# Attention layer and four-way state-space layer on one core: one frame for the sums of D, turned copies in 2 KB runs ordered during the scans

## The chip, the cores and the metric

The kernel runs on one core of a Trainium2 chip. The metric is device time in microseconds (us), from start to end of one execution. The engines are PE (TensorE, matrix products; PEld is its weight load), DVE (VectorE), ACT (ScalarE), POOL (GpSimd) and SP (SyncE, which issues most DMAs). Each works through its own queue in order. "DVEq", "POOLq" and the like are an engine's sequencer: waits and issues.

## The reference, cut to what matters

```python
# layer 0, on x of (B, H, W, C) = (8, 128, 128, 128)
q, k, v = split(x @ w_qkv)                      # 4 heads of 32, N = H*W tokens
q = softmax(q over the 32) / sqrt(32);  k = softmax(k over N)
context = einsum('bhdn,bhen->bhde', k, v)
out = einsum('bhde,bhdn->bhen', context, q) @ w_out + b_out
x1 = layernorm(out) + x

# layer 1, on x1
xb, z = split(x1 @ Win)                         # 256 channels each
u = silu(conv3x3_depthwise(xb))                 # in the code: xb
xs = [u by rows, the same reversed, u by columns, the same reversed]   # K = 4 orders
dt, B, C = split(xs_flat @ Wxproj)              # 8 + 1 + 1 rows per image and order
delta = softplus(dt_weight @ dt + dt_bias)
# the (image, order) axis of u, B, C and dt is reshaped from (8, 4) to (4, 8), so output image o, slot s
# takes image o // 4 + 2 * s in order o % 4
h[t] = exp(delta[t] * A) * h[t-1] + delta[t] * u[t] * B[t];  y[t] = h[t] * C[t] + u[t] * D
y = y_0 + reversed(y_1) + turned(y_2) + turned(reversed(y_3))
out = (layernorm(y * silu(z)) * gamma + beta) @ Wout
```

"Turned" means that the two axes of the 128 x 128 image change places.

## The kernel before

The kernel has three parts in sequence. All images are held with channels on the 128 partitions. The layout NAT runs through an image column by column (the input arrives with w ahead of h), TURN row by row.

**layer0** does the attention image by image, in `ORDER`, with 32 groups of 512 tokens (4 columns) per image. While one image is in `attend`, the next is in `context`; the stages of both are interleaved by hand in `image`, and `in_order` keeps each engine's instructions in the written order. Between images, `gate` projects x to z for the gating of layer 1: per group two matrix products, a silu on ACT, and two stores of 256 KB to `zs`; after that (or, for images that are not turned, in eight pieces meanwhile) it loads the image after the next. For images with `ORDER[b] % K >= 2` DVE first makes a turned copy `v` of the group. `finish` makes x1 and stores two groups at a time. The last two images have their gate groups spread through the last pass.

**layer1_front** takes x1 through the projection, the 3 x 3 depthwise convolution and silu, in `SEQ` order of images (4, 6, 5, 7, 0, 1, 2, 3), 16 steps of 1024 tokens (8 columns) each, for both halves c of 256 channels. Two of the nine taps are on PE (`taps_pe`), three on ACT with POOL adding (`taps_act`), four on DVE (`taps_dve`). `rows` and `keep_rows` make the ten rows of dt, B and C; `by_b` multiplies u by B and stores it in NAT order to `ubs`. A whole image of u stays in SBUF (`ures`). Eight steps later and on, `turn` copies it turned, in pieces of 16 rows by 64 columns, two pieces (`ka`, `kb`) a step, and `store_turned` writes each piece to the TURN half of `ubs`. `copy_on` says which engine copies. `split_step` turns the ten rows (`turn_rows`) and splits them in both orders into three bf16 parts (`split`), two rows at a time.

`sum_d` makes D * u on ACT. The sums of D over the four images that meet in one output are gathered in DRAM: images 4 to 7 go to `gts` in blocks of 8 x 8, and images 0, 1 read them back (`load_sum`), add them on POOL, and store the result to `gs`, to which images 2, 3 add by an accumulating DMA from POOL's queue (`add_sum`).

**layer1_scan** runs over 8 output images x 4 slots x 16 units of 1024 tokens. A unit makes delta (PE, ACT), the product with u (`weigh`, on POOL, in place in `ubt`), the scan itself (DVE), the product by C (`emit`, DVE) and the addition to y (`gather` on DVE, `add` on POOL). The slot at place 0 starts an image's y; meanwhile the image before leaves: `gate`, moments, `project`, `store`. `add_d` adds the sums of D to y by an accumulating DMA from POOL's queue. In `step` the order of every engine is again written out by hand.

Two lines carry much of what follows: the product in place, and a turned piece's 64-element runs in DRAM.

```python
nc.gpsimd.tensor_tensor(ubt[n][:, c, :], ubt[n][:, c, :], sp.pop((n, c)), ALU.mult)      # weigh
nc.sync.dma_start(dst[:, 16 * i : 16 * i + 16, hf * HALF : hf * HALF + HALF], turned.pop(k))   # store_turned
```

Of the kernel before, what the change touches and what calls it, by code (L numbers as in the profile page):

```python
# [16 lines left out]
P = 128  # L17
# [11 lines left out]
ORDER = (2, 3, 6, 7, 4, 5, 0, 1)  # L29
# [11 lines left out]
def split3(eng, parts, x, copy):  # L41

    for j in range(3):
        copy(parts[j], x)
        if j < 2:
            eng.tensor_tensor(x, x, parts[j], ALU.subtract)
# [31 lines left out]
def layer0(ctx: ExitStack, tc, xT, w_qkv, w_out, b_out, gamma, beta, win, x1, zs):  # L78
# [68 lines left out]
    def gate_group(b, g):  # L147

        v = group(b, g)
        if ORDER[b] % K >= 2:  # L150
            v = wp.tile([P, GW, P], F32, name="v", tag="o", bufs=3)
            nc.vector.tensor_copy(
                v, xs[b % 2].rearrange("p w h -> p h w")[:, g * GW : (g + 1) * GW, :]
            )
        for c in range(NC2):
            pz = ps.tile([P, GW, P], F32, name="pz", tag="ps")
            nc.tensor.matmul(pz, wz[:, c * P : c * P + P], v, start=True, stop=True)
            z = wp.tile([P, GW, P], F32, name="z", tag="k", bufs=7)
            nc.scalar.activation(z, pz, AF.Silu)
            dst = zs[ORDER[b], c][:, g * GN : g * GN + GN]  # L160
            nc.sync.dma_start(dst, z.rearrange("p w h -> p (w h)"))

    def gate(b):

        turned = ORDER[b] % K >= 2
        more = b + 2 < B
        for g in range(NG):
            gate_group(b, g)
            if more and not turned and g % 4 == 3:
                load(b + 2, [g // 4])  # L170
        if more and turned:
# [89 lines left out]
    def attend(b):  # L261
# [61 lines left out]
        def finish(g):  # L323
# [4 lines left out]
            if g % 2 == 1:  # L328
# [55 lines left out]
def layer1_front(ctx: ExitStack, tc, x1, win, conv_w, conv_b, wxp, d_par, ubs, xds, xps, gts, gs):  # L384
# [19 lines left out]
    ON_PE = ((1, -1), (1, 1))  # L404
    ON_ACT = ((-1, -1), (-1, 0), (-1, 1))
    ON_DVE = ((0, -1), (0, 0), (0, 1), (1, 0))
# [3 lines left out]

    ident = const.tile([P, P], F32, name="ident1")
    make_identity(nc, ident)
    cw = const.tile([P, NC2, 9], F32, name="cw")
# [45 lines left out]
    SEQ = (4, 6, 5, 7, 0, 1, 2, 3)  # L459

# [3 lines left out]
    accs, sums, pxs, prs, pbs, gls, dus = {}, {}, {}, {}, {}, {}, {}  # L464
# [42 lines left out]
    def taps_act(n, c):  # L507
        for j, d in enumerate(ON_ACT):
# [4 lines left out]
            nc.scalar.activation(t, at(n, c, *d), AF.Copy, scale=cw[:, c, tap(*d) : tap(*d) + 1])  # L513
# [5 lines left out]
    def taps_dve(n, c):  # L519
        acc = accs[n, c]  # L520
        nc.vector.tensor_tensor(acc, sums.pop((n, c)), acc, ALU.add)  # L521
        for d in ON_DVE:
            nc.vector.scalar_tensor_tensor(  # L523
                acc, at(n, c, *d), cw[:, c, tap(*d) : tap(*d) + 1], acc, ALU.mult, ALU.add
            )
# [27 lines left out]
    def by_b(n):  # L553

        b, g = place_of(n)
        dst = ubs[b, NAT].rearrange("c p l -> p c l")
# [6 lines left out]
    def sums_at(n, c):  # L563
        b, g = place_of(n)
        i = NCH - 1 - g if b // 2 % 2 == 1 else g
        if b >= 4:
            return gts[b % 2, c, :, i].rearrange("p e q -> p (e q)")
        return gs[b % 2, c][:, i * CH : i * CH + CH]

    def load_sum(n, c):  # L570
        b, g = place_of(n)
        if b // 2 == 0:
            gls[n, c] = gl = wp.tile([P, CH], F32, name="gl", tag="d", bufs=2)
            nc.sync.dma_start(gl.rearrange("p (e q) -> p e q", e=NCH), gts[b % 2, c, :, :, g])

    def sum_d(n):
        b, g = place_of(n)
        s = b // 2
        for c in range(NC2):
            u = ures[:, c, g * CH : g * CH + CH]  # L580
            if s == 0:
                dus[n, c] = t = wp.tile([P, CH], F32, name="du", tag="tb", bufs=4)
                nc.scalar.activation(t, u, AF.Copy, scale=sd[:, s, c : c + 1])
                gl = gls.pop((n, c)).rearrange("p (e h) -> p h e", h=8)
                tw = t.rearrange("p (w h) -> p w h", w=CW)
                nc.gpsimd.tensor_tensor(tw, tw, gl, ALU.add)
                continue
            dus[n, c] = t = wp.tile([P, CH], F32, name="du", tag="d", bufs=2)
            dst = t[:, ::-1] if s % 2 == 1 else t
            if s >= 2:  # L590
                u = u.rearrange("p (w i h) -> p w i h", w=CW, h=8)
                dst = dst.rearrange("p (i w h) -> p w i h", w=CW, h=8)
            nc.scalar.activation(dst, u, AF.Copy, scale=sd[:, s, c : c + 1])

    def store_sum(n):
        s = place_of(n)[0] // 2
        if s % 2 == 0:
            for c in range(NC2):
                nc.sync.dma_start(sums_at(n, c), dus.pop((n, c)))

    def add_sum(n):
        s = place_of(n)[0] // 2
        if s % 2 == 1:
            for c in range(NC2):
                nc.gpsimd.dma_start(sums_at(n, c), dus.pop((n, c)), accum_op=ALU.add)
# [6 lines left out]
    def turn(k, copy, tag, bufs):  # L612
        m, r = divmod(k, COPIES)
        b, hf = SEQ[m // 2], m % 2
        c, i = divmod(r, COPIES // NC2)
        turned[k] = t = wp.tile([P, 2 * 8, HALF], F32, name="turned", tag=tag, bufs=bufs)
        copy(t, uturn[:, c, 16 * i : 16 * i + 16, hf * HALF : hf * HALF + HALF])

    def store_turned(k):
# [3 lines left out]
        dst = ubs[b, TURN][c].rearrange("p (h w) -> p h w", w=W)  # L623
        nc.sync.dma_start(dst[:, 16 * i : 16 * i + 16, hf * HALF : hf * HALF + HALF], turned.pop(k))

    def dve_copy(out, x):
        nc.vector.scalar_tensor_tensor(out, x, 1.0, x, ALU.mult, ALU.max)

    def copy_on(n, second):
        s = place_of(n)[0] // 2 if n < N else 2  # L630
        if s == 0:
            return nc.scalar.copy if second else dve_copy if n % 2 else nc.gpsimd.tensor_copy
        if s % 2 == 1 and second:
            return dve_copy if n % 2 else nc.scalar.copy
        return nc.gpsimd.tensor_copy
# [4 lines left out]
    def load_rows(q, r0, rows, tag, bufs):  # L640
        x = wp.tile([P, rows, H], F32, name="xw", tag=tag, bufs=bufs)
        xws[q, r0] = x
# [3 lines left out]
    def turn_rows(q, r0, rows, tag, bufs):  # L646
        x = xws[q, r0]
        pt = (pm if rows <= 4 else pj).tile([P, rows, P], F32, name="ptx", tag="m" if rows <= 4 else "pj")
        for j in range(rows):
            nc.tensor.transpose(pt[:, j, :], x[:, j, :], ident)  # L650
        y = wp.tile([P, rows, W], F32, name="xh", tag=tag, bufs=bufs)
        nc.scalar.copy(y, pt)
        xws[q, r0, TURN] = y

    def split(q, r0, rows, order, eng, tag, bufs):
        v = xws.pop((q, r0, TURN) if order == TURN else (q, r0))
        p = wp.tile([P, 3, rows, P], BF16, name="parts", tag=tag, bufs=bufs)
        split3(eng, [p[:, j] for j in range(3)], v, dve_copy if eng is nc.vector else eng.tensor_copy)
        parts.append((q, r0, rows, order, p))

    def store_parts():
        while parts:
            q, r0, rows, order, p = parts.pop()
            dst = xps[SEQ[q], order].rearrange("j r (a e) -> a j r e", e=P)
# [3 lines left out]
    def split_step(n):  # L668
# [6 lines left out]
        eng = nc.vector if place_of(n)[0] // 2 == 0 else nc.gpsimd  # L675
        if odd:
            turn_rows(q, 2 * j, 2, "sy", 1)
            split(q, 2 * j, 2, NAT, eng, "sq", 1)
        else:
            if j:  # L680
                split(q, 2 * j - 2, 2, TURN, eng, "sq", 1)
# [3 lines left out]
    def step(n):  # L685
# [6 lines left out]
        if ka >= 0:  # L692
            turn(ka, copy_on(n, False), "tc", 2)
# [15 lines left out]
        if live:  # L709
            for c in range(NC2):  # L710
                load_sum(n, c)
        if ka - 1 >= 0:
            store_turned(ka - 1)
# [566 lines left out]
```

## Time and profile before

| | |
|---|---|
| median of 3 runs | 9476.79 us (9473.5 to 9477.35) |
| profiled execution | 9477.74 us, span 9475.9 us |
| busy share of PE, DVE, ACT, POOL | 67%, 86%, 75%, 79% |
| DMA packets | 1,510,245, of them 799,444 under 512 bytes |
| bytes moved | 1784 MB, mean 188 GB/s |

The profile is of one execution. A group's row gives line, engine, operation, tiles (out<-in), shapes and count; then the busy us, the mean ns of one, and after the second bar the idle us just before its instructions and what ended them. "Windows" give the busy time of each engine between two times. The DMA share is that of 16 DMA engines.

### The profile page before, as it was taken

How to read it: one execution, taken by the hardware profiler on the slowest of the kernel's cores; microseconds unless marked ns; L12 is line 12 of the kernel's file. 1: busy time of each engine (PE TensorE's matmuls, PEld its weight loads, DVE VectorE, ACT ScalarE, POOL GpSimd, SP SyncE). 2: the span in 40 equal slices, each digit the busy share in tenths (PEclk: the TensorE clock that was granted, in tenths of full speed). 3: DMA queues.
4: the chain of work that ended last, by engine and by line, in shares of the span. 5: the costliest groups of instructions: out<-in, count | busy, mean ns of one | idle time of the engine just before them, and what ended most of it. 6: DMA issues, size and time to landing. Idle time of an engine off the chain costs nothing. (4 is left out here: it accounts for less than half of the span.)

```text
span 9475.9 us, 89695 instructions
## 1 busy us (share of the span) xinstructions
PE 6389.1 (67%) x24352; PEld 3122.5 (33%) x24352; DVE 8149.5 (86%) x8046; ACT 7125.4 (75%) x8034; POOL 7474.3 (79%) x4743
## 2 busy tenths in 40 slices
PE   8999999898989887788633644637345363543636
PEld 5555555564333332233200311304023040320403
DVE  6667765563999999999789999999999999999996
ACT  5556655567888887788678888888878888888884
POOL 3445544455789987788769999999999999999997
PEclk9999999999999998899855755758566585665857
DMA  2331233314598898999955958769586685967858
GB/s 92 134 134 71 106 134 132 133 63 152 180 230 244 231 231 229 233 232 224 226 158 171 273 154 228 223 181 264 158 238 203 190 256 166 247 187 201 248 163 214
DMA packets 1510245, 1784.08 MB, mean 188 GB/s; under 512 B 799444, under 2 KB 1025364, under 8 KB 1501552
## 3 DMA queue, kind: packets, MB, share of 16 engines
q1 hardware_dynamic: 1456496, 1577.01, 53.5%
q0 software_dynamic: 53248, 201.34, 11.4%
q8 instruction: 199, 3.26, 0.1%
q14 instruction: 302, 2.47, 0.1%
HBM read 1085.92 MB, written 692.12 MB: 188 GB/s over the span
## 5 line engine op out<-in xcount | busy, mean ns | idle before, releaser
L963 POOL TENSOR_TENSOR ubt<-ubt,sp 128x1024 f32<-128x1024 f32 x1024 | 2458.0, 2458 | 160.0 <-ACT sp L956 96.1
L952 PE MATMUL px<-rows,dtw 128*128 128x512 bf16 x2048 | 953.6, 565 | 2238.4 <-DVE y L1013 1069.2
L515 POOL TENSOR_TENSOR tap<-tap 128x1024 f32<-128x1024 f32 x512 | 1261.4, 2468 | 234.3 <-ACT tap L513 209.2
L523 DVE SCALAR_TENSOR_TENSOR acc<-xb,cw,acc 128x1024 f32<-128x1024 f32 x1024 | 1320.6, 1290 | 54.0 <-ACT xb L492 1.7
L956 ACT ACTIVATE sp<-px 128x1024 f32<-128x1024 f32 x1024 | 1046.2, 1024 | 418.1 <-PE px L952 351.0
L1021 POOL TENSOR_TENSOR y<-y,ubt 128x512 f32<-128x512 f32 x768 | 1155.3, 1550 | 146.0 <-DVE ubt L994 144.9
L505 PE MATMUL acc<-xi,wt 128*128 128x512 f32 x2048 | 1028.1, 648 | 314.3 <-ACT ures L530 314.3
L973 DVE TENSOR_TENSOR_SCAN ubt<-px,ubt 128x1024 f32<-128x1024 f32 x512 | 1176.9, 2332 | 27.4 <-POOL ubt L963 20.3
L971 DVE TENSOR_TENSOR_SCAN ubt<-px,ubt 128x1024 f32<-128x1024 f32 x512 | 1178.4, 2332 | 13.1 <-POOL ubt L963 6.0
L952 PEld LDWEIGHTS <-dtw 128*128 128x128 bf16 x2048 | 164.6, 109 | 3065.9 <-issue 869.7
L960 ACT ACTIVATE px<-sp,sa 128x1024 f32<-128x1024 f32 x1024 | 1110.1, 1109 | 6.1
L513 ACT ACTIVATE tap<-xb,cw 128x1024 f32<-128x1024 f32 x768 | 828.3, 1140 | 134.9 <-DVE acc L521 85.4
L282 POOL TENSOR_TENSOR q<-q,qs 128x512 f32<-128x512 f32 x256 | 271.7, 1061 | 698.2 <-DVE qs L281 698.2
L956 ACT ACT_TABLE_LOAD x512 | 656.9, 1283 | 169.6 <-PE px L952 146.9
L505 PEld LDWEIGHTS acc<-xi,wt 128*128 128x128 f32 x2048 | 398.1, 205 | 917.6 <-issue 497.1
L960 ACT ACT_TABLE_LOAD x512 | 656.9, 1283 | 9.0
L1086 PEld LDWEIGHTS px<-wg,z 128*128 128x128 f32 x4096 | 556.6, 219 | 117.9 <-issue 112.7
L979 PE MATMUL pc<-rows,csel 128*128 128x512 bf16 x1024 | 515.8, 584 | 81.3 <-DVE rstd L1074 77.5
L1086 PE MATMUL px<-wg,z 128*128 128x128 f32 x4096 | 556.7, 302 | 0.0
L478 PE MATMUL pxb<-xi,wi 128*128 128x512 f32 x1024 | 483.7, 595 | 10.1 <-DMA xi<-x 7.9
L1013 DVE TENSOR_TENSOR y<-y,px 128x1024 f32<-128x1024 f32 x384 | 468.7, 1221 | 14.4
L298 ACT ACTIVATE sq<-o 128x512 f32<-128x512 f32 x256 | 161.2, 630 | 420.1 <-DVE o L296 418.9
(160 smaller groups left out, 15379.7 us busy)
## 6 DMA issues: line engine op xcount, KB each, us to landing
ubt<-ubs SPq DMA_DIRECT2D x512, 1024.0 KB
zs<-z SPq DMA_DIRECT2D x512, 256.0 KB
ubs<-ures SPq DMA_DIRECT2D x256, 512.0 KB
ubs<-turned SPq DMA_DIRECT2D x256, 512.0 KB
z<-zs SPq DMA_DIRECT2D x256, 512.0 KB
y<-gs POOLq DMA_DIRECT2D x128, 1024.0 KB, 10.4
rows<-xps SPq DMA_DIRECT2D x1536, 60.0 KB
xi<-x SPq DMA_DIRECT2D x120, 576.0 KB
```

The source lines that it names most:

```text
L505: nc.tensor.matmul(acc[:, s, :], wt[:, j, c, :], x, start=(j == 0), stop=(j == len(ON_PE) - 1))
L513: nc.scalar.activation(t, at(n, c, *d), AF.Copy, scale=cw[:, c, tap(*d) : tap(*d) + 1])
L515: nc.gpsimd.tensor_tensor(sums[n, c], sums[n, c], t, ALU.add)
L523: nc.vector.scalar_tensor_tensor(acc, at(n, c, *d), cw[:, c, tap(*d) : tap(*d) + 1], acc, ALU.mult, ALU.add)
L952: nc.tensor.matmul(p[:, hf * 512 : hf * 512 + 512], sl.dw[:, c * P : c * P + P], src, start=True, stop=True)
L956: nc.scalar.activation(t, da[n, c], AF.Softplus)
L960: nc.scalar.activation(da[n, c], sp[n, c], AF.Exp, scale=sa[:, sl.s, c : c + 1])
L963: nc.gpsimd.tensor_tensor(ubt[n][:, c, :], ubt[n][:, c, :], sp.pop((n, c)), ALU.mult)
L971: nc.vector.tensor_tensor_scan(e[:, ::-1], x[:, ::-1], e[:, ::-1], start, ALU.mult, ALU.add)
L973: nc.vector.tensor_tensor_scan(e, x, e, start, ALU.mult, ALU.add)
L1021: nc.gpsimd.tensor_tensor(v[:, c], v[:, c], h[:, c], ALU.add)
L1086: nc.tensor.matmul(po[:, w, :], z[:, c, w * H : w * H + H], wg[:, c, :], start=(c == 0), stop=(c == NC2 - 1))
```

## The change

In layer 0 the images are taken in the order 0, 1, 4, 5, 2, 3, 6, 7. Images 0 to 3 are written to x1 in turned order, from a DVE copy in the gate, in place of the store in `finish`; images 0, 1, 4, 5 are projected to z from a turned copy. All loads of the image after the next follow the gate. In the front, images 0 to 3 are thus held in TURN order as their own order, with the taps' weights exchanged to match, and the sums of D of all eight images lie in one frame: images 4, 5 are stored to `gs`, the others are added by DMA, both halves of channels in one, from one buffer. `gts` and the addition on POOL are gone. The tap (0, 0) goes from DVE to PE and (1, -1) from PE to DVE. Turning copies are on POOL; outside images 4 and 5 the second one of a step is shared, half by POOL and half by ACT. A turned piece is stored in runs of 2 KB, in an order that isn't quite the scan's. In the scans, `weigh` reads u in the missing order, for the slots whose order isn't the image's own, and writes a tile `h` of its own. u is loaded per half of channels, two units ahead in place of three, after the `weigh` that frees its buffer. The bf16 parts are split once, on POOL, and the parts are turned on PE.

```diff
-ORDER = (2, 3, 6, 7, 4, 5, 0, 1)
+ORDER = (0, 1, 4, 5, 2, 3, 6, 7)
...
     def gate_group(b, g):
         v = group(b, g)
-        if ORDER[b] % K >= 2:
-            v = wp.tile([P, GW, P], F32, name="v", tag="o", bufs=3)
+        if ORDER[b] % K < 2 or ORDER[b] < B // 2:
+            t = wp.tile([P, GW, P], F32, name="v", bufs=4)
             nc.vector.tensor_copy(
-                v, xs[b % 2].rearrange("p w h -> p h w")[:, g * GW : (g + 1) * GW, :]
+                t, xs[b % 2].rearrange("p w h -> p h w")[:, g * GW : (g + 1) * GW, :]
             )
+            if ORDER[b] < B // 2:
+                nc.sync.dma_start(x1[ORDER[b]][:, g * GN : g * GN + GN], t.rearrange("p w h -> p (w h)"))
+            if ORDER[b] % K < 2:
+                v = t
...
         for g in range(NG):
             gate_group(b, g)
-            if more and not turned and g % 4 == 3:
-                load(b + 2, [g // 4])
-        if more and turned:
+        if b + 2 < B:
             load(b + 2)
...
-            if g % 2 == 1:
+            if g % 2 == 1 and ORDER[b] >= B // 2:
...
-    ON_PE = ((1, -1), (1, 1))
+    ON_PE = ((0, 0), (1, 1))
...
-    ON_DVE = ((0, -1), (0, 0), (0, 1), (1, 0))
+    ON_DVE = ((0, -1), (0, 1), (1, -1), (1, 0))
...
+    def own(b):
+        return TURN if b < B // 2 else NAT
...
+    SEQ_FIRST = (4, 5)
...
     def sum_d(n):
         b, g = place_of(n)
         s = b // 2
+        dus[n] = t = wp.tile([P, NC2, CH], F32, name="du", tag="d", bufs=1)
         for c in range(NC2):
...
+            dst = t[:, c, ::-1] if s % 2 == 1 else t[:, c, :]
+            nc.scalar.activation(dst, ures[:, c, g * CH : g * CH + CH], AF.Copy, scale=sd[:, s, c : c + 1])
...
     def add_sum(n):
-        s = place_of(n)[0] // 2
-        if s % 2 == 1:
-            for c in range(NC2):
-                nc.gpsimd.dma_start(sums_at(n, c), dus.pop((n, c)), accum_op=ALU.add)
+        if place_of(n)[0] not in SEQ_FIRST:
+            nc.gpsimd.dma_start(sums_at(n), dus.pop(n), accum_op=ALU.add)
...
     def store_turned(k):
...
-        dst = ubs[b, TURN][c].rearrange("p (h w) -> p h w", w=W)
-        nc.sync.dma_start(dst[:, 16 * i : 16 * i + 16, hf * HALF : hf * HALF + HALF], turned.pop(k))
...
+        dst = ubs[b, 1 - own(b)][c].rearrange("p (g e q) -> p g e q", e=2, q=8 * HALF)[:, 2 * i : 2 * i + 2, hf, :]
+        nc.sync.dma_start(dst, turned.pop(k).rearrange("p (g h) w -> p g (h w)", g=2))
...
-            turn(kb, copy_on(n, True), "tc", 2)
+            turn(kb, [nc.gpsimd.tensor_copy, nc.scalar.copy] if shared(n) else [nc.gpsimd.tensor_copy], "tc", 2)
...
+    def turn_parts(q, r0, rows, tag, bufs):
+        p = xws.pop((q, r0))
+        pt = (pm if rows <= 2 else pj).tile([P, 3, rows, P], BF16, name="ptx", tag="m" if rows <= 2 else "pj")
+        for j in range(3):
+            for r in range(rows):
+                nc.tensor.transpose(pt[:, j, r, :], p[:, j, r, :], ident16)
+        y = wp.tile([P, 3, rows, P], BF16, name="xh", tag=tag, bufs=bufs)
         nc.scalar.copy(y, pt)
...
         if odd:
-            turn_rows(q, 2 * j, 2, "sy", 1)
-            split(q, 2 * j, 2, NAT, eng, "sq", 1)
+            split(q, 2 * j, 2, nc.gpsimd, "sq", 1)
         else:
             if j:
-                split(q, 2 * j - 2, 2, TURN, eng, "sq", 1)
+                turn_parts(q, 2 * j - 2, 2, "sy", 1)
...
+            self.permuted = self.order != (TURN if self.b < B // 2 else NAT)
...
-        for s in ([3, 0, 1, 2] if o % 4 < 2 else [1, 2, 3, 0]):
+        for s in ([3, 0, 1, 2] if o % 4 >= 2 else [1, 2, 3, 0]):
...
     def weigh(n, c):
-        nc.gpsimd.tensor_tensor(ubt[n][:, c, :], ubt[n][:, c, :], sp.pop((n, c)), ALU.mult)
+        if c == 0:
+            hs[n] = wp.tile([P, NC2, CH], F32, name="h", bufs=2)
+        u, t, h = ubt.pop((n, c)), sp.pop((n, c)), hs[n][:, c, :]
+        if units[n][0].permuted:
+            u = u.rearrange("p (e h w) -> p h e w", e=2, w=W // 2)
+            t, h = (v.rearrange("p (h e w) -> p h e w", e=2, w=W // 2) for v in (t, h))
+        nc.gpsimd.tensor_tensor(h, u, t, ALU.mult)
...
-        start = 0.0 if i == 0 else ubt[n - 1][:, c, last : last + 1]
+        start = 0.0 if i == 0 else hs[n - 1][:, c, last : last + 1]
...
             weigh(n, 0)
+            if n + 2 < N:
+                load(n + 2, 0)
...
-            if n + 3 < N:
-                load(n + 3)
```

## The prediction

> **What bounds the kernel now.** I read the page's 40 slices first, then busy time by stage, by image and by slot, then groups and waits inside a stage.
>
> ```profile
> DVE  6667765563999999999789999999999999999996
> POOL 3445544455789987788769999999999999999997
> DMA  2331233314598898999955958769586685967858
> ```
> Three stages: layer 0 to slice 10, the front of layer 1 to slice 20, the scans after. In the last two VectorE (DVE) is at nine tenths; in the front the DMA engines are as well.
>
> ```profile
> 0.00:2367.00 2367.00, 2134.47 (x9408) 1302.89 (x9408) 1494.15 (x2600) 1437.09 (x2438) 1162.93 (x1292) 0.98 0.30 115
> 2367.00:4760.00 2393.00, 1943.88 (x4696) 746.63 (x4696) 2181.85 (x1733) 1897.58 (x2012) 1983.55 (x1141) 0.93 0.87 225
> 4760.00:9476.00 4716.00, 2310.73 (x10248) 1072.94 (x10248) 4473.49 (x3717) 3790.76 (x3584) 4327.84 (x2312) 0.63 0.71 207
> ```
> Columns: window and length, then busy us of PE, weight load, DVE, ACT, POOL, then clock, DMA share, GB/s. Layer 0 is PE's (90%), the scan is DVE's (95%) with POOL at 92%. Inside:
>
> ```profile
> 2906.40:3156.10 249.70, 229.80 (x579) 88.62 (x578) 238.04 (x193) 216.92 (x239) 236.33 (x152) 0.99 0.83 249
> 3156.10:3445.20 289.10, 246.06 (x598) 93.93 (x597) 260.95 (x201) 240.20 (x258) 253.83 (x169) 0.96 0.91 222
> 3445.20:3779.00 333.80, 251.32 (x573) 96.68 (x571) 316.49 (x251) 243.87 (x250) 267.99 (x107) 0.88 0.90 232
> ...
> 5605.90:5737.40 131.50, 46.76 (x97) 9.03 (x96) 129.21 (x81) 108.31 (x96) 125.22 (x64) 0.50 0.57 176
> 5737.40:5870.70 133.30, 47.31 (x103) 9.83 (x106) 129.37 (x82) 110.18 (x98) 127.45 (x75) 0.50 0.79 211
> ```
> The first three rows are front images 5, 7, 0, of 16 steps each: 15.6, 18.1, 20.9 us a step. Image 5 has no copies or splits on DVE; its 14.9 us of DVE a step is the convolution and the product by B. Image 7 adds every fourth turning copy on DVE, image 0 that and the bf16 splits. By the distance of each image's first convolution sums, the eight images (order 4, 6, 5, 7, 0, 1, 2, 3) take 15.3, 17.5, 15.6, 18.1, 20.9, 21.1, 18.2, 17.4 us a step. The last two rows are slots at places 2 and 3 of an image in the scan: 8.22 and 8.33 us a unit.
>
> What is slow inside image 7, then image 0, then the slot at place 2:
>
> ```profile
> L627 DVE SCALAR_TENSOR_TENSOR turned<-ures 128x1024 f32<-128x1024 f32 x8 | 23.3, 2916 | 20.3 <-DMA ubs<-turned 17.7 <-issue 2.6
> L605 POOL DMA_DIRECT2D gts<-du x30 | 26.6, 1022 | 0.5 <-ACT du L593 0.3 <-issue 0.2
> ```
> ```profile
> L586 POOL TENSOR_TENSOR du<-du,gl 128x1024 f32<-128x1024 f32 x30 | 90.9, 3054 | 29.9 <-ACT du L583 29.9
> ```
> ```profile
> L963 POOL TENSOR_TENSOR ubt<-ubt,sp 128x1024 f32<-128x1024 f32 x32 | 74.8, 2363 | 0.0
> L1021 POOL TENSOR_TENSOR y<-y,ubt 128x512 f32<-128x512 f32 x32 | 51.3, 1629 | 6.3 <-DVE ubt L994 6.3
> ```
> DVE not only spends 2.9 us on a turning copy, it also waits for the store of an earlier one, 17.7 us in the image. In the scan POOL needs 2 x 2.36 + 2 x 1.63 = 7.98 of the 8.22 us: slack 0.24.
>
> **What the Trainium skill says.** "DMA: Bandwidth & Descriptors", Specifications, asks for transfers of at least 512 B for line rate. The trace agrees: a 256 B packet takes 0.0195 us around 3500 us, which is 210 GB/s on 16 engines, a 2 KB one 0.090 us, 364 GB/s. The same page, "Issuing engines are not separate DMA queues": sums moved from SP's queue to POOL's gain no bandwidth; the trace shows one shared total, 91% in image 7. "GPSIMD Engine Reference", 7 (Performance pitfalls for Q7 kernels): an inner step above 8 bytes costs about half as much again per element. L586 (step 32 bytes in one operand) agrees in kind: 3.05 us where contiguous operands take 2.36. The same page, 8 (Key points): GpSimd shares SBUF interfaces with DVE. The 128x256 split copy on DVE takes 423 ns in one place and 1757 in another of image 0, which fits.
>
> **The change, part by part**, against the profiled execution's 9477.7 us (1.8 more than its span; the median shown is 9476.8).
>
> Layer 0, gates. Slots 0 and 1 of the order (images 0, 1) now also store x1 inside the gate from DVE copies; so do images 2, 3 at positions 4, 5, which had no copies and loaded the next image meanwhile. Positions 2, 3 stay as they were in kind. Gate windows, with copies, then without:
>
> ```profile
> 337.80:400.00 62.20, 57.24 (x128) 25.30 (x129) 27.72 (x40) 39.57 (x65) 1.65 (x1) 0.95 0.69 258
> ...
> 1484.50:1552.00 67.50, 60.47 (x129) 25.37 (x128) 3.25 (x8) 36.21 (x62) 1.05 (x1) 0.92 0.90 312
> ```
> A gate stores 16.8 MB of z; x1 makes it 25.2. At full DMA share the rows give 258/0.69 = 374 and 312/0.90 = 347 GB/s, so 67 to 73 us; I take 70, against 57 and 67.4. The load of the next image comes behind that backlog: up to 7 z and 4 x1 tiles of 262 KB, 7.7 us, taken as 4, on top of the 4.6 us for which PE already waits after a gate. Positions 0, 1: 13 + 4 each; positions 4, 5: 2.6 + 8.6 each. Sum **+56**, between +29 (67 us, no backlog) and +82 (both upper ends). The 64 added DVE copies (0.75 us) lie under PE's matmuls in the gate; without that cover they cost 48.
>
> Front. DVE loses its turning copies and all step splits, so every image has image 5's 14.9 us. POOL there: 14.8, less half a copy (1.0) and less five of ten splits (5 x 2.55/16 = 0.8), plus one accumulating DMA of 1 MB (1.25 for the same form in the scan, y<-gs): 14.3. ACT: 13.6, plus half a copy (1.0) and a wider copy of turned parts (0.14): 14.7. PE stays at 14.4; the centre tap only changes places with (1,-1). DMA in image 7: 0.91 x 18.1 = 16.4 us a step, less 4096 x 0.0195/16 = 5.0, plus 512 x 0.090/16 = 2.9: 14.3. Images 0, 1 lose also the gts reads and POOL's 3.05 us adds. All five resources stand below image 5's 15.6. What becomes late next is du: one buffer for both halves. After the ACT writes it, POOL does one and a half turning copies (3.0 us) before it issues the addition, which lands 10.4 us later (the page's y<-gs median): 13.4, just when ACT wants the buffer again (15.6 - 2.3 = 13.3). In five of 16 steps a split of 2.55 stands in between as well; half of it absorbed, that is 0.4 a step. ACT's next taps are queued behind that wait, and POOL's adds wait for them. So **16.0** us for six images: 96 x 16.0 = 1536 against 113.2 x 16 = 1811, -275; images 4, 5 -3. Bounds: 15.4 (landing early, -333) and 17.2 (landing always near 13, -160).
>
> Tail. SP issues the remaining turned stores:
>
> ```profile
> 4701.56 34.98 SPq L624 DMA_DIRECT2D ubs<-turned  x15
> ```
> 2.3 us each; with 2 KB packets 0.52 MB/364 GB/s = 1.4, saving 13. Half of 20 DVE split instructions of 0.83 go, 8. Taken **-20**, from -25 to 0.
>
> Scan. `weigh` writes a new tile h (two buffers) and, at places 1 and 2 only, reads u in runs of 64. Those runs are contiguous, so I take 2.36 us and no cost; the upper end is L586's 3.05. New wait: weigh(n) cannot write before scan(n-1) has read h of n-2, where POOL used to run ahead by about 1.3 us. Behind it on POOL stand the rstd pair, gate and adds, and DVE waits for both products. From that moment the first product is needed 3.66 us on (three DVE passes), and takes 2.4; so at places 1, 2 nothing is lost. At places 0 and 3, where POOL also issues additions of D, it smooths less: 0.1 us x 256 units, **+25**, from -10 (less waiting of DVE for output stores) to +60. SP now waits for each product before loading two units ahead; out stores are behind that, but they wait for later DVE work anyway.
>
> Sum: +56 - 278 - 20 + 25 = -217, hence **9260**.
>
> **Rivals.** (a) The forecast, 0.60.
> (b) Slower: POOL pays for the permuted read at places 1 and 2. At 3.05 us its unit is 9.36 against 8.22, x 256 units = +292: 9552. It decides from (0.24 + 217/256)/2 = 0.54 us more a product, 2.90. For it: POOL has 3% of slack there. Against it: it is the step that costs in L586. 0.13.
> (c) The DMA queues keep the front: 17.2 us a step, no gain in the tail, +82 in layer 0: 9478 - 163 + 82 + 25 = 9422. For it: 14.3 us of transfers a step and a single du. 0.17, of which 0.05 ends near zero.
> (d) Everything hides: 15.4 us, +29, tail -25, scan 0: 9478 - 336 - 25 + 29 = 9146. 0.10.
> That the runs stay 256 B is excluded by the DMA's shape, 128 x 2 x 512.
>
> **The numbers.** A measurement here can tell about 0.2% (19 us). Faster by more 0.82 (a, d, most of c), same 0.05, slower 0.13 (b). Range 9160 to 9470: it leaves out b and the far end of d.
>
> **What would show it.** Packets under 512 B fall from 799,444 by 655,360 (256 x 2048 turned, 64 x 2048 gts). Front steps of images 6, 7, 0 to 3 near 16; gates of four images near 70 us; weigh at 2.4 us. Wrong if weigh at places 1 and 2 exceeds 2.5, if "du <- DMA gs" waits exceed 1 us a step, or if the front stays over 17.

## The result, and the profile after

The changed kernel takes 9365.94 us (median of 4 runs, 9360.47 to 9382.31) against 9476.14 for the kernel before on the same chip: a ratio of 0.9888, 95% interval 0.9874 to 0.9903. That is 110 us faster, where the prediction said 217. The profiled execution took 9364.78 us with a span of 9363.0.

From the page of the changed kernel, the 40 slices of three rows and the packets:

```profile
DVE  6667666674799988888799999999999999999996
POOL 3446444465688888888589899998999989999997
DMA  1322333223477788888757759578595785967858
DMA packets 934771, 1750.67 MB, mean 187 GB/s; under 512 B 150229, under 2 KB 376149, under 8 KB 926065
```

In the front (slices 11 to 20) the DMA engines are no longer at nine tenths, and DVE is in three slices only, where it was in all but one; in the scans little looks different. Packets under 512 bytes fell by 649,215. The same by stage, from the windows (from, to, length; busy us of PE, weight load, DVE, ACT, POOL with instructions; clock, DMA share, GB/s). The borders are the first convolution sums on DVE, the last ones, and the first scan:

```profile
0.00:2407.40 2407.40, 2152.88 (x9437) 1300.19 (x9438) 1545.65 (x2671) 1442.20 (x2443) 1167.22 (x1296) 0.97 0.29 113
2407.40:4516.10 2108.70, 1875.58 (x4769) 720.17 (x4769) 1898.89 (x1522) 1837.39 (x2020) 1777.60 (x1054) 0.98 0.79 230
4516.10:4610.80 94.70, 23.74 (x76) 9.94 (x73) 42.40 (x57) 29.85 (x26) 33.39 (x27) 0.58 0.72 224
4610.80:9219.40 4608.60, 2215.29 (x9338) 1034.26 (x9337) 4448.49 (x3541) 3743.36 (x3516) 4242.94 (x2251) 0.61 0.71 204
```

Against the same events in the trace of before:

| part | before | after | difference | forecast |
|---|---|---|---|---|
| layer 0, to the first sums of the front | 2380.7 | 2407.4 | +26.7 | +56 |
| front, first to last sums | 2287.5 | 2108.7 | -178.8 | -278 |
| tail, to the first scan | 114.5 | 94.7 | -19.8 | -20 |
| scans and end | 4693.2 | 4752.2 | +59.0 | +25 |

The front misses by 99 us, the scans by 34, layer 0 by 29 the other way. Images 5, 7 and 0 of the front, to be read against the same three images before:

```profile
2921.50:3170.50 249.00, 232.44 (x610) 90.35 (x610) 238.55 (x193) 222.69 (x246) 227.32 (x128) 1.00 0.73 256
3170.50:3440.40 269.90, 237.31 (x603) 91.05 (x602) 239.78 (x193) 233.30 (x258) 229.19 (x142) 0.97 0.83 232
3440.40:3712.70 272.30, 239.30 (x607) 91.84 (x608) 240.15 (x193) 235.28 (x260) 230.75 (x143) 0.97 0.84 232
```

That is 15.6, 16.9 and 17.0 us a step (before 15.6, 18.1, 20.9). The six images with the shared copy take 16.7, 16.9, 17.0, 16.9, 17.1 and 17.3, 17.0 in the mean. In image 0 DVE needs 15.0, ACT 14.7, POOL 14.4, PE 15.0, and the DMA engines 14.3 us a step: these are near their forecasts (PE, at 15.0 where 14.4 was forecast, is the farthest off), and no engine fills the step. What an engine waits for in the image after it, image 1 (us in total, times, longest):

```profile
POOL tap L525 <- ACT tap L523: 33.5, 30, 2.3
ACT xb L497 <- PE pxb L488: 31.6, 15, 3.1
PE acc L515 <- ACT ures L538: 28.1, 16, 2.1
...
ACT du L582 <- DMA gs<-du: 0.3, 1, 0.3
```

The wait for the single `du` buffer, on which the forecast of 16.0 was built, is 0.3 us in sixteen steps, and the additions land 8.8 us after their issue (median), not 10.4. ACT and PE wait for each other in nearly every step. One step of ACT, then PE at that moment, from the timeline of image 1 (start, duration, instructions; in brackets the idle time ahead):

```profile
3749.35 2.19 ACT L582 ACTIVATE du<-ures,sd 128x1024 f32<-128x1024 f32 x2
3751.44 1.06 ACT L605 COPY turned<-ures 128x512 f32<-128x512 f32 x1
...
3757.35 1.11 ACT L538 ACTIVATE ures<-acc,cb 128x1024 f32<-128x1024 f32 x1
3758.36 3.22 ACT L523 ACTIVATE tap<-xb,cw 128x1024 f32<-128x1024 f32 x3
3761.48 1.10 ACT L538 ACTIVATE ures<-acc,cb 128x1024 f32<-128x1024 f32 x1
3764.69 1.01 ACT L497 COPY xb<-pxb 128x1024 f32<-128x1024 f32 x1 [2.11 <-PE pxb L488]
```
```profile
3758.51 3.70 PE L515 MATMUL acc<-xi,wt 128*128 128x512 f32 x8 [1.65 <-ACT ures L538]
3762.70 1.96 PE L488 MATMUL pxb<-xi,wi 128*128 128x512 f32 x4 [0.48 <-DMA xi<-x]
```

This is a ring. The silu on ACT (`ures`) frees the convolution's accumulator; only then does PE start the next taps, and behind them the projection; only then can ACT place it (`xb`). From 3757.35 to 3764.69 the ring is set by PE and ACT idles 2.1 us. In PE's part stands a short wait for the load of x1, 0.48 us here and 4.2 us in the whole image. For the rest of the step ACT works without a gap: `xb`, `du`, the half turning copy, `xd`, taps, again to `ures`. So a step is ACT's 14.7 us plus those 2 us. If this reading of the trace is right, what stands on ACT between `xb` and `ures` lengthens the step, though ACT has idle time. The experiments test that.

### The profile page after: what moved, and what is told of

The parts are those of the page before. It is cut to its first block, busy times and chain, and to the rows that moved or that the text cites. A ratio compares the mean times of both kernels' runs of the same rounds, so it can differ in the third digit from the quotient of the medians.

```text
span 9363.0 us, 91413 instructions
## 1 busy us (share of the span) xinstructions
PE 6381.8 (68%) x24512; PEld 3145.7 (34%) x24512; DVE 7997.6 (85%) x7953; ACT 7096.1 (76%) x8066; POOL 7319.3 (78%) x4684
## 3 DMA queue, kind: packets, MB, share of 16 engines
q0 software_dynamic: 60928, 234.90, 13.5%
## 5 line engine op out<-in xcount | busy, mean ns | idle before, releaser
L946 POOL TENSOR_TENSOR h<-ubt,sp 128x1024 f32<-128x1024 f32 x1024 | 2416.1, 2388 | 371.0 <-DMA rows<-xps 110.2
L525 POOL TENSOR_TENSOR tap<-tap 128x1024 f32<-128x1024 f32 x512 | 1211.2, 2366 | 299.1 <-ACT tap L523 278.8
L956 DVE TENSOR_TENSOR_SCAN h<-px,h 128x1024 f32<-128x1024 f32 x512 | 1177.8, 2332 | 32.0 <-ACT px L937 15.7
L954 DVE TENSOR_TENSOR_SCAN h<-px,h 128x1024 f32<-128x1024 f32 x512 | 1178.5, 2332 | 21.3 <-POOL h L946 18.4
L1004 POOL TENSOR_TENSOR y<-y,h 128x512 f32<-128x512 f32 x768 | 1158.6, 1550 | 3.9 <-DVE h L977 3.9
L515 PE MATMUL acc<-xi,wt 128*128 128x512 f32 x2048 | 985.4, 625 | 194.8 <-ACT ures L538 194.8
L523 ACT ACTIVATE tap<-xb,cw 128x1024 f32<-128x1024 f32 x768 | 825.2, 1140 | 16.7 <-POOL xb L499 16.5
L1069 PEld LDWEIGHTS px<-wg,z 128*128 128x128 f32 x4096 | 595.9, 232 | 114.1 <-issue 108.0
L1069 PE MATMUL px<-wg,z 128*128 128x128 f32 x4096 | 594.3, 315 | 0.0
L488 PE MATMUL pxb<-xi,wi 128*128 128x512 f32 x1024 | 487.2, 598 | 39.1 <-DMA xi<-x 36.9
L996 DVE TENSOR_TENSOR y<-y,px 128x1024 f32<-128x1024 f32 x384 | 468.7, 1221 | 14.4
```

Source lines behind the costliest of these rows:

```text
L515: nc.tensor.matmul(acc[:, s, :], wt[:, j, c, :], x, start=(j == 0), stop=(j == len(ON_PE) - 1))
L523: nc.scalar.activation(t, at(n, c, *d), AF.Copy, scale=weight(n, c, *d))
L525: nc.gpsimd.tensor_tensor(sums[n, c], sums[n, c], t, ALU.add)
L946: nc.gpsimd.tensor_tensor(h, u, t, ALU.mult)
L954: nc.vector.tensor_tensor_scan(e[:, ::-1], x[:, ::-1], e[:, ::-1], start, ALU.mult, ALU.add)
L956: nc.vector.tensor_tensor_scan(e, x, e, start, ALU.mult, ALU.add)
```

## The experiments

Ratios are to the kernel before, in the same session (its medians 9468 to 9476). Differences "to the changed kernel" are between the two ratios, times 9476. Where two values stand beside one another, the changed kernel's is given as such.

### What sets the front's step

**e1: both turning copies on POOL.**

```diff
-turn(kb, [nc.gpsimd.tensor_copy, nc.scalar.copy] if shared(n) else [nc.gpsimd.tensor_copy], "tc", 2)
+turn(kb, [nc.gpsimd.tensor_copy], "tc", 2)
```

> The changed kernel with both turning copies of a step on POOL in all images (ACT's half copy undone). Theory ACT-PE ring: in the shared images a step (16.9 us) is one turn of ACT: silu of half 0, PE taps and projection (3.7 + 1.9 us), ACT's place, D*u, half copy, taps, place, next silu; the 1.07 us of half copy lie in that ring, so the six images fall to about 15.9 us a step and the time by 70 to 100 us, to about 9265 to 9295. Rival, the prediction's: one du buffer and the landing of the additions bind; POOL then issues the addition 1.0 us later, so a step grows by 0.5 to 1.0 us and the time by 50 to 95 us. Second rival, POOL binds with the copy back on it (14.4 + 1.0 = 15.4 us): a step near 16.5, the time down by about 40 us.

Measured 9294.47 us, 0.9812 (0.9796 to 0.9829), 72 us below the changed kernel. The front takes 2051.7 us (changed kernel 2108.7), the six images 15.9 to 16.6 a step, 16.4 in the mean. In image 1:

```profile
3681.40:3946.70 265.30, 235.60 (x607) 89.90 (x606) 239.41 (x193) 222.09 (x245) 245.78 (x143) 0.99 0.86 239
```

ACT lost 0.8 us a step, and the mean step of the six images fell by 0.6, in image 1 by 0.3. ACT's wait for `du` (`ACT du <- DMA gs`), which the forecast feared, appears now that ACT has less to do and POOL issues the addition later: 47.7 us in the front, 9.1 of them in image 1, where the changed kernel has 1.3 and 0.3. POOL gained 0.9 us a step and is at 93%. Of the 72 us the trace gives 57 to the front. One image met the 15.9 us that was expected; the mean is nearer to the second rival's 16.5, with POOL next to bound.

**e6: the second copy wholly on ACT**, the opposite.

```diff
-turn(kb, [nc.gpsimd.tensor_copy, nc.scalar.copy] if shared(n) else [nc.gpsimd.tensor_copy], "tc", 2)
+turn(kb, [nc.scalar.copy] if shared(n) else [nc.gpsimd.tensor_copy], "tc", 2)
```

> The changed kernel with the second copy of a step wholly on ACT in the shared images (half of it on POOL before). Theory ACT-PE ring: ACT's part grows by 0.9 us and so does the step, from 16.9 to 17.7 to 17.9, the time by 75 to 95 us, to 9440 to 9460. Rival, POOL or its issue of the additions binds: POOL has 1.1 us less, the step falls. Rival, DMA binds: no change.

Measured 9479.32 us, 1.0012 (1.0005 to 1.0019): the whole gain is gone. Image 1, window and wait:

```profile
3773.50:4067.00 293.50, 247.85 (x606) 95.46 (x606) 240.47 (x193) 249.35 (x260) 214.31 (x126) 0.94 0.78 215
```
```profile
ACT xb L497 <- PE pxb L488: 40.9, 15, 4.5
```

ACT is busy 15.6 us of an 18.3 us step (changed kernel 14.7 of 16.9), 0.9 more, and the step grew by 1.4, more than the 0.8 to 1.0 that was expected; ACT's wait for PE took the other 0.6. In this image PE is busy 247.9 us at a granted clock of 0.94, against 238.9 at 0.97 for as many products, 0.56 us a step; whether that is cause or consequence of the longer step isn't shown. DVE, POOL, PE and the DMA engines are all less full than in the changed kernel. With e1 this shows that ACT's work passes into the step though ACT is busy for only 85% of it.

**e9: the second half of the copy on DVE.**

```diff
-turn(kb, [nc.gpsimd.tensor_copy, nc.scalar.copy] if shared(n) else [nc.gpsimd.tensor_copy], "tc", 2)
+turn(kb, [nc.gpsimd.tensor_copy, nc.vector.tensor_copy] if shared(n) else [nc.gpsimd.tensor_copy], "tc", 2)
```

> The changed kernel, with the second half of the shared turning copy on DVE in place of ACT. Theory (the chain of taps and waits through ACT sets the front's step): ACT loses 1.07 us a step, DVE goes from 14.9 to about 15.7, so the step falls from 16.9 to 16.0 to 16.3 in the six shared images: 60 to 90 us faster than the changed kernel, 9275 to 9305. Rival 1 (DVE and POOL delay each other when both copy, or DVE waits for the store of an earlier piece as it did before the change): the copy of 512 takes 1.5 us or more on DVE and the step stays at 16.8 or goes over 17: 9360 to 9400. Rival 2 (the du buffer, as predicted, binds as soon as ACT is relieved): steps of about 16.5 with over 0.5 us of du <- DMA gs each.

Measured 9305.78 us, 0.9825 (0.981 to 0.9839), 60 us below the changed kernel. Image 1, window and then the copy's row:

```profile
3691.60:3954.80 263.20, 234.30 (x610) 89.05 (x609) 254.34 (x210) 223.20 (x244) 236.35 (x143) 1.00 0.87 242
```
```profile
L605 DVE COPY turned<-ures 128x512 f32<-128x512 f32 x17 | 18.9, 1114 | 1.9 <-DMA ubs<-turned 1.8
```

The step is 16.45 us, and DVE is busy for 15.9 of it. The copy costs 1.1 us on DVE, as on ACT. DVE's busy time rose by 0.9 us a step where 0.8 was expected, and the step stayed above the 16.0 to 16.3 expected. ACT's wait for PE (`xb`) fell from 31.6 to 8.6 us in the image, and ACT waits for DVE's sums instead (`ures <- DVE acc`, 28.0 us): the ring of ACT and PE is nearly off the path, and DVE takes over at once.

**e5: D * u ahead of the placing**, in the time in which ACT idles.

```diff
             silu(n, 1)
+        if live:
+            sum_d(n)
         if later:
             place(n + 2, 0)
         if live:
             rows(n)
-            sum_d(n)
```

> The changed kernel with ACT's two D*u instructions of a step put ahead of its place of step n+2, half 0, so that they fill the 2 us in which ACT waits for PE's projection. Theory ACT-PE ring: the ring loses those 2.2 us, ACT has 14.8 us of work and 0 to 0.5 of waits, the six images fall from 16.9 to 15.6 to 16.0 us a step, the time by 85 to 125 us, to 9240 to 9280. Rival, the prediction's: with one du buffer the D*u instructions, now earlier in the step, wait for the landing of the addition (8.8 us after issue), and the step falls by less than 0.4 us, the time by under 40. Rival, DMA at 0.84 share binds: no change.

Measured 9335.14 us, 0.985 (0.9835 to 0.9865), 36 us below the changed kernel: a third of what was expected. The steps are 16.6 to 16.9. Image 1:

```profile
ACT xb L497 <- PE pxb L488: 18.1, 18, 1.6
...
ACT du L582 <- DMA gs<-du: 9.3, 5, 2.2
```

The wait for PE fell from 31.6 to 18.1 us, but `du` is now written earlier, and its buffer is not always back: 9.3 us in the image, 62.8 in the whole front (1.3 in the changed kernel). Of the 13.5 us that ACT won in the image, `du` took 9.0 back, and the image is 3.6 us shorter. So the mechanism of the forecast exists; it stands behind the ring, and the time is the one that the first rival of this run gave (under 40 us). What keeps the remaining 18.1 us wasn't taken apart, and that a shorter ring alone shortens the step is shown only for these few us.

**e2: PE's projection ahead of its taps**, to shorten PE's part of the ring.

```diff
-        if then:
-            taps_pe(n + 1, 0)
         if later:
             project(n + 2, 0)
+        if then:
+            taps_pe(n + 1, 0)
```

> The changed kernel with PE's projection of step n+2, half 0, put ahead of its taps of step n+1, half 0. Theory ACT-PE ring: ACT's wait for that projection (about 2 us a step in the shared images, 31.6 us in image 1) goes; the six images fall from 16.9 to between 15.3 and 15.9 us a step, the time by 95 to 150 us, to 9215 to 9270. Rival (DMA or the du buffer binds): the wait moves to another row and the time stays within 20 us. Second rival: the projection, issued earlier, now waits for the load of xi, and PE's taps behind it with it: the time grows.

Measured 9532.24 us, 1.006 (1.0045 to 1.0075): slower, with 18.8 us a step. Image 1:

```profile
DVE acc L531 <- PE acc L515: 48.7, 11, 8.7
PE pxb L488 <- DMA xi<-x: 48.5, 15, 7.0
```

The projection, asked for earlier, waits for the load of x1, and the taps that DVE needs are now queued behind it. The second rival of this run held. PE's part of the ring has thus not been shortened by any run; that it belongs to the ring is read from the trace.

**e11: the turned pieces in runs of 256 bytes again**, and the product in the scan without its permutation. Do the 2 KB runs make the front faster?

```diff
-        dst = ubs[b, 1 - own(b)][c].rearrange("p (g e q) -> p g e q", e=2, q=8 * HALF)[:, 2 * i : 2 * i + 2, hf, :]
-        nc.sync.dma_start(dst, turned.pop(k).rearrange("p (g h) w -> p g (h w)", g=2))
+        dst = ubs[b, 1 - own(b)][c].rearrange("p (h w) -> p h w", w=W)
+        nc.sync.dma_start(dst[:, 16 * i : 16 * i + 16, hf * HALF : hf * HALF + HALF], turned.pop(k))
```

> The changed kernel, but turned pieces are stored in their true order in runs of 256 bytes as before the change, and the product in the scan reads u straight. Theory (the front's step is set by engines, and transfers are below it): transfers go from 14.3 to 16.4 us a step under a step of 16.9, so the step rises by 0.3 to 1 us: +30 to +100 us in the front and +13 in the tail, nothing in the scan: 9400 to 9480. Rival 1 (the 2 KB runs are what made the front faster): steps of over 18, above 9500. Rival 2 (runs do not matter): steps within 0.1 us, only the tail, 9375 to 9385.

Measured 9376.04 us, 0.9904 (0.9887 to 0.992): the interval overlaps the changed kernel's. By the trace the front takes 2102.3 us (changed kernel 2108.7), the tail 114.7 (changed kernel 94.7). Image 1, and then the fifteen last turned stores on SP, of e11 and of the changed kernel:

```profile
3704.00:3975.80 271.80, 239.30 (x604) 91.55 (x603) 240.13 (x193) 235.31 (x260) 230.98 (x143) 0.97 0.95 233
```
```profile
4544.80 35.15 SPq L612 DMA_DIRECT2D ubs<-turned  x15
```
```profile
4547.58 18.82 SPq L612 DMA_DIRECT2D ubs<-turned  x15
```

The DMA share rises from 0.84 to 0.95 at the same step: 1.9 us more of transfers a step cost nothing under the ring. The second rival of this run held, not its theory. Without the longer runs the tail is as long as before the change (114.5 us).

**e8: the kernel before with 2 KB runs alone.** The scans read those pieces in the order stored; putting u in order is left out.

```diff
-        dst = ubs[b, TURN][c].rearrange("p (h w) -> p h w", w=W)
-        nc.sync.dma_start(dst[:, 16 * i : 16 * i + 16, hf * HALF : hf * HALF + HALF], turned.pop(k))
+        dst = ubs[b, TURN][c].rearrange("p (g e q) -> p g e q", e=2, q=8 * HALF)[:, 2 * i : 2 * i + 2, hf, :]
+        nc.sync.dma_start(dst, turned.pop(k).rearrange("p (g h) w -> p g (h w)", g=2))
```

> The kernel before with its turned pieces stored in runs of 2 KB and nothing else; the scans then read u of the TURN slots in a wrong order, so the output differs from the reference. It prices the 2 KB runs alone. Theory: the front before is bound by DVE (copies and splits), and of the transfers only the waits of DVE and POOL for stores of turned pieces count, about 1 to 1.5 us a step in six images, and 13 us in the tail: 90 to 150 us less, about 9325 to 9385. Rival, the front before is bound by its DMA engines (0.90 to 0.94 share): the 2.1 us less of transfers a step come off in full, 200 us or more. Second rival: DVE's own work binds alone: only the tail's 13 us.

Measured 9442.72 us, 0.9968 (0.9956 to 0.998). The front gains 15.6 us (2287.5 in before, 2271.9 here), the tail 14.7. Image 1:

```profile
3758.30:4096.30 338.00, 252.12 (x591) 95.80 (x590) 315.49 (x252) 252.22 (x260) 276.12 (x109) 0.89 0.83 236
```

DVE stays at 93% of a step of 21.1 us. The forecast of 90 to 150 us failed; its second rival, DVE's own work binding, is the nearest. (The trace shows layer 0, whose code is the same, 10.0 us shorter as well.) What the front gained in the change is thus for the most part DVE's relief, not the DMA engines'.

### What the scans lose

At place 0 the sum over eight images rose from 1370.8 to 1416.8 us, at place 3 from 1056.0 to 1071.0; places 1 and 2 changed by 1.2 us or less. DVE's rows and waits in the second image's slot at place 0, before and then in the changed kernel (`z` is the gate's product; `r` is the output tile, which waits until an earlier store of it has landed):

```profile
L1041 DVE TENSOR_TENSOR z<-y,z 128x1024 f32<-128x1024 f32 x15 | 27.8, 1850 | 0.0
DVE r L1092 <- DMA out<-r: 4.0, 3, 1.9
L1024 DVE TENSOR_TENSOR z<-y,z 128x1024 f32<-128x1024 f32 x15 | 33.4, 2229 | 0.0
DVE r L1075 <- DMA out<-r: 9.1, 6, 2.3
```

Such rows, summed over the eight images at place 0 (us), with three of the runs below that change something there:

| | length | DVE busy | of that, gate products | DVE waits for output stores |
|---|---|---|---|---|
| before | 1370.8 | 1297.4 | 195.4 | 32.8 |
| changed kernel | 1416.8 | 1338.7 | 237.0 | 39.1 |
| e3 | 1426.5 | 1285.4 | 178.3 | 71.9 |
| e4 | 1370.3 | 1343.4 | 247.0 | 2.7 |
| e10 (e3, e4, e9) | 1347.2 | 1300.3 | 201.6 | 8.7 |

So of the 46 us that place 0 lost, 41 are DVE's busy time, and those are the gate's products; the waits for output stores account for 6. The length has some scatter: over the seven runs with the changed kernel's scan it is 1400 to 1417 us.

**e3: the scan's starting value copied to a small tile on ACT**, so that POOL's product doesn't wait for the next scan to read `h`.

```diff
-        last = 0 if sl.back else CH - 1
-        start = 0.0 if i == 0 else hs[n - 1][:, c, last : last + 1]
+        start = 0.0 if i == 0 else carries[n - 1][:, c, :]
...
+    def carry(n):
+        last = 0 if units[n][0].back else CH - 1
+        carries[n] = t = sm.tile([P, NC2, 1], F32, name="carry")
+        nc.scalar.copy(t, hs[n][:, :, last : last + 1])
...
+        if live:
+            carry(n)
```

> The changed kernel in which ACT copies the last column of each unit's scan to a small tile, from which the next scan starts, so that the buffer of h comes free one scan earlier and POOL can run ahead again. Theory: the new wait makes POOL's first product start together with DVE's gate at place 0, and the two slow each other (DVE's gate 2.34 us where it took 1.85 to 1.96 before); with the wait gone the gate is back below 2.0, place 0 falls from 11.6 to about 11.2 us a unit, place 3 from 8.45 to 8.33: 45 to 60 us less, about 9305 to 9320. Rival: the place 0 units are long because output stores land late behind the loads of u that are now issued ahead of them: under 15 us less, and the waits of DVE for output stores stay.

Measured 9369.76 us, 0.989 (0.9876 to 0.9905): no difference. Place 3 falls back from 8.45 to 8.33 us a unit, 15 us in all, but place 0 stays at 1426. The table shows both halves of that. The gate's products fall from 237 to 178 us, so the new wait is what had made them slow: in the traces POOL's own products run during 38% of their time before the change, 55% in the changed kernel, 37% in e3. But DVE's waits for output stores rise from 39 to 72 us, and nothing is gained. The theory was right on the products and wrong on the time; the time is the rival's.

**e4: u loaded at the end of the step, behind the output stores.**

```diff
             weigh(n, 0)
-            if n + 2 < N:
-                load(n + 2, 0)
...
             weigh(n, 1)
-            if n + 2 < N:
-                load(n + 2, 1)
...
+        if n + 2 < N:
+            for c in range(NC2):
+                load(n + 2, c)
```

> The changed kernel with the loads of u for unit n+2 issued by SP at the end of step n, behind the output stores, where the kernel before had its load. Rival of the POOL wait: output stores are late because they stand behind those loads; then the waits of DVE for output stores at place 0 (9.1 us in one slot, 4.0 before) fall to about 4 and the time by 25 to 45 us. Theory (POOL's new wait): the gate on DVE stays at 2.34 us and the time changes by under 15 us.

Measured 9322.16 us, 0.9841 (0.9826 to 0.9856), 45 us below the changed kernel. The waits for output stores are gone (2.7 us), and place 0 is back at 1370.3. That it is back at the time of before is a coincidence: the gate's products stay slow (247 us), and most of the waits removed were there before the change (32.8 us). SP's queue at place 0, changed kernel and then e4:

```profile
5167.16 1.84 SPq L1020 DMA_DIRECT2D z<-zs  x2
5169.10 3.54 SPq L918 DMA_DIRECT2D ubt<-ubs  x2
5172.73 1.21 SPq L1079 DMA_DIRECT2D out<-r  x2
```
```profile
5163.85 2.17 SPq L1020 DMA_DIRECT2D z<-zs  x2
5167.99 1.41 SPq L1079 DMA_DIRECT2D out<-r  x2
5169.49 1.23 SPq L918 DMA_DIRECT2D ubt<-ubs  x2
```

In the changed kernel the stores of the output leave behind two loads, each of which waits for POOL's product to free its buffer. In the slot shown DVE waits 9.1 us for output buffers (`DVE r <- DMA out<-r`), 1.6 us in e4. DVE's busy time is the same in both, 175.3 and 175.8 us, in a slot of 189.9 and 180.9. The granted clock of PE is also lower in the slower slot (0.83 and 0.92); the edit moves only the loads, and what the clock adds isn't shown.

### Together

**e7: e4 and e5.** The two diffs above.

> The two together: loads of u at the end of the scan's step, and D*u ahead of place in the front. They lie in different stages; if both causes are right the gains add: 9366 less 44 (measured for the loads alone) less 85 to 125: 9195 to 9240. If the ring is wrong: 9320.

Measured 9290.75 us, 0.981 (0.9794 to 0.9826): -74 us to the changed kernel where the parts give -45 and -36. Within the intervals they add.

**e12: e4, e5 and e9.** The three diffs above.

> The changed kernel with u loaded behind the output stores, the D * u products ahead of the taps of the placing stage on ACT, and the shared half copy on DVE in place of ACT. If the earlier D * u and the lighter ACT help separately, gains add: -44 -31 -60 to -90: 9200 to 9230. If both only shorten the same chain through ACT, the second brings nothing: 9235 to 9260, front steps equal to those with the half copy on DVE alone.

Measured 9273.34 us, 0.9791 (0.9777 to 0.9806). The front takes 2063.1 us against 2057.5 in e9: with DVE at the bound the earlier D * u brings nothing that can be seen, as the second case said (e10, whose front is e9's, took 2067.1).

**e10: e4, e3 and e9.** The three diffs above.

> Three repairs of the changed kernel at once: u is loaded at the end of a scan step, behind the output stores; the scan's starting value is copied to a small tile on ACT, so that POOL's product has not to wait for the next scan; the shared half copy is on DVE in place of ACT. If the causes are separate, the gains add: -44 (place 0), -15 (place 3), -60 to -90 (front): 9215 to 9250. If the two repairs in the scan concern the same time, 9225 to 9265. If DVE's half copy does not help the front, about 9305.

Measured 9225.1 us, 0.9741 (0.9727 to 0.9756): the fastest version, 139 us below the changed kernel. The front gives 41 us, place 3 15, place 0 70 (from 1416.8 to 1347.2). At place 0 the repairs do more than add: e3 alone gave nothing, e4 alone 46. In e4 seven of the images stand between 178.8 and 180.9 us at place 0; with the copied start value as well they take 173.0 to 178.7. The gate's products are back near their time of before (201.6 us) and the waits for output stores stay small (8.7). So the wait for `h` costs time at place 0 too: e4 removed one of two delays, and with e3 alone the other took what was won.

## Why the prediction was right or wrong

**The direction and the mechanism of the gain** were right. DVE's turning copies and splits bound the front, and the change took them away; e8 shows that the shorter transfers alone did little. The busy times per step came as forecast, all but PE's within 0.1 us, and packets under 512 bytes fell by nearly the number forecast (655,360).

**The step that failed is the 16.0 us of the six shared images.** It took image 5's step, 15.6, as the largest load, with a small wait for `du` on top. The images take 17.0. At 95 steps between their sums the 1.0 us is 93 us, nearly the whole miss of the front. The sum treated ACT's 14.7 us as work that lies beside 15.6, so that the half copy given to ACT cost the step nothing. In its place the runs show the ring: ACT's 14.7 us and the 2 us for which it waits for PE in each step. The image that the forecast started from already waited in a circle. The waits of image 5 in the kernel before:

```profile
ACT ures L530 <- DVE acc L523: 19.7, 15, 2.1
...
PE acc L505 <- ACT ures L530: 14.6, 16, 2.2
```

ACT waits for DVE's sums and PE for ACT's silu, once in nearly every step. Such a line says that work added to ACT may lengthen the step, and the forecast didn't read it. Worked out afterwards, image 5's 15.6 plus the half copy's 1.06 is 16.6; images 6 and 7 take 16.7 and 16.9. e6 and e1 showed that work on ACT passes into the step in both directions, e6 by more than its size and e1 by less. The forecast's own test, "du <- DMA gs" over 1 us a step, came out at 0.02; the wait that it feared stands behind the ring and shows in e1 and e5. Rival (c), DMA queues at 17.2, has nearly the right number for the wrong reason: e11 puts 1.9 us of transfers on a step and moves nothing.

**Scans, +25 forecast, +59.** The product through the permutation costs nothing that can be seen, as said, which ends rival (b). POOL's rows in the slot at place 2, to be read against the same rows before (2363 and 1629 ns):

```profile
L946 POOL TENSOR_TENSOR h<-ubt,sp 128x1024 f32<-128x1024 f32 x33 | 77.0, 2354 | 5.8 <-DMA rows<-xps 3.7 <-DVE h L954 1.1 <-DMA dtw<-wparts 0.6
L1004 POOL TENSOR_TENSOR y<-y,h 128x512 f32<-128x512 f32 x32 | 51.8, 1645 | 0.0
```

The wait for the next scan was forecast at 0.1 us x 256 units at places 0 and 3. At place 3 it is 0.12 us x 128, 15 us, shown by e3. At place 0 the term failed: 0.36 us x 128. It counted how long DVE would wait for POOL, and not that POOL's product, once moved, would run beside DVE's gate and slow it: 41 us more of DVE's busy time, which the same wait causes, as e3 and e10 show. The prediction had named such slowing, in its reading of the split copies, and put none in the sum. A sentence failed as well, that output stores behind SP's waits cost nothing since "they wait for later DVE work anyway". They leave late and DVE runs out of output buffers; in the changed kernel this hides what e3 would gain, and e4, which ends it, gives 46 us.

**Layer 0, +56 forecast, +27.** Gate windows after, first slot, second slot, then position 4:

```profile
337.90:407.00 69.10, 61.87 (x129) 23.90 (x130) 27.53 (x40) 39.58 (x66) 1.65 (x1) 0.95 0.87 332
642.80:707.00 64.20, 61.45 (x128) 23.71 (x129) 23.67 (x31) 37.44 (x63) 0.79 (x1) 0.96 0.94 356
1508.50:1570.00 61.50, 59.37 (x130) 22.89 (x129) 26.56 (x40) 36.20 (x61) 1.34 (x1) 1.00 0.91 344
```

At full share these are 378 to 382 GB/s, above the 347 to 374 assumed. From its first product's start to its last one's, PE's gate takes 63.4 and 64.0 us at positions 0 and 1, where 70 was taken: with the late loads +13 and +11 in place of 17 each. At positions 4 and 5 the term was wrong in kind: the gate lost the loads it had carried and fell from 67.4 to 60.7 us, while PE waits longer for x afterwards (all such waits of layer 0 rose from 33.1 to 68.1 us), and from one of these gates to the next nothing changed (294.6 us before, 294.3 after). This row is known to some 10 us only: layer 0 of before's code took 2380.7 us and, in e8, 2370.7, and that of the changed kernel between 2398.8 and 2410.4 over its runs. That the miss here goes the other way and takes 29 us off the total miss is luck.

**Tail, -20:** measured -19.8, but the split of 13 for the runs and 8 for DVE's splits isn't what the runs show. The longer runs alone bring 14.7 us in the kernel before (e8), and with the rest of the change in place they are worth all of it (e11), so the shares depend on the order; that the sum fits is partly luck.

## What to carry to other kernels

When no engine fills a step, write down the ring: who waits for whom in every step, and whose work lies on it; work moved to an engine with idle time lengthens the step if it lies on the ring, here by 0.6 us (e1) to 1.4 us (e6) for 0.8 to 0.9 us of work. When a load gets a later condition, look at what stands behind it in the issuing queue: a store that "waits anyway" is what frees the next buffer. Two delays in series hide one another, so a repair that shows nothing alone (e3 at place 0) is tried again once the other is gone; and a repair that brings the old time back (e4) need not have undone what the change did: compare the engine's busy time and its waits apart.

## What the runs showed of the hardware

- A POOL product that reads one operand in runs of 64 elements costs the same as a straight one: 2354 ns against 2363 in the kernel before, and in e11, which reads straight, the mean at place 2 is the same 2353 ns. The Trainium skill, "GPSIMD Engine Reference", 7 (Performance pitfalls for Q7 kernels), warns of inner steps above 8 bytes; here the inner step stays 4 bytes, and the trace shows no penalty.
- In e11 packets of 256 bytes in place of 2 KB took the DMA share of a step from 0.84 to 0.95 and cost no time until the tail, where 15 stores of 0.52 MB took 35.2 us of SP's queue in place of 18.8.
- The DVE gate product took 1850 ns in one slot at place 0 before the change and 2229 ns after it, with more of POOL's product beside it; over the seven images that have it the means are 1861 and 2258 ns, and 1699 and 1920 ns in e3 and e10, which move POOL's product away again. In e4 it stayed slow (2352 ns) and was not hidden: DVE is busy for 175.8 of the 180.9 us of that slot.
